# Two reorderings in a transformer block: token sums over other rows, and norms one group of sums later

## The chip, the cores and the metric

The kernel runs on one core of a Trainium2 chip. The metric is the device time of one execution in microseconds, the median of several runs; lower is better. The engines named below are TensorE (PE in the profile; PEld is its weight load), VectorE (DVE), ScalarE (ACT), GpSimd (POOL) and SyncE (SP). The last two, and sometimes ScalarE, also issue transfers between the on-chip memory (SBUF) and DRAM. TensorE writes its results to another on-chip memory, PSUM, from which VectorE or ScalarE takes them.

## The reference

One block of a diffusion transformer, in float32, on `x` of shape (2, 2048, 576) with a condition vector for each of the two sequences. Cut to what matters:

```python
mod = silu(c) @ w_ada + b_ada
sh_msa, sc_msa, g_msa, sh_mlp, sc_mlp, g_mlp = split(mod, 6, axis=1)
xn = ln(x) * (1 + sc_msa) + sh_msa
q, k, v = split_heads(xn @ w_qkv + b_qkv)          # 16 heads of 36
q, k = ln(q), ln(k)
o = softmax(q @ k.T * scale) @ v                   # over all 2048 tokens
x = x + g_msa * (o @ w_proj + b_proj)              # "projection"
xn2 = ln(x) * (1 + sc_mlp) + sh_mlp
h = gelu(xn2 @ w1 + b1)                            # 576 -> 2304
x = x + g_mlp * (h @ w2 + b2)
```

The line marked "projection" and the layer norm of the line after it are what the change concerns.

## The kernel before

The program has two branches; the profiled one is `block_of_small`. It treats the two sequences b = 0 and b = 1 in turn: inputs (norm, q, k, v), attention, projection. Then comes the MLP over all 4096 tokens, in two parts: `w1` with the gelu, whose results go to DRAM, and `w2`. A token tile is 128 rows of 576 numbers; a sequence has 16 tiles. In the MLP a block is 512 tokens. A job makes two slices of 128 hidden features for one block, and does so with seven products of half size in place of eight; there are 8 blocks of 9 jobs.

Instructions of an engine run in the order in which they stand in the program. TensorE's order is the order of the source throughout the branch. VectorE's is the order of the source in the two projections and from the second one to the end; there a list of closures (`between`, `placed`) is the only thing that puts other work into it. ScalarE, GpSimd and SyncE are ordered by a scheduler there. A wait is set for the engine wherever a buffer's last user has to be done, including transfers that still read a buffer which is to be overwritten.

**Projection (`outputs`, L1250 on).** Sixteen tiles in groups of four. For a tile, `whole` (L413) multiplies the attention output by the first 512 rows of `w_proj`, and `halved` (L424) by the last 64. TensorE's order in a group is: `whole` of tiles 0 and 1, `halved` of all four, `whole` of tiles 2 and 3. Each tile takes one of four PSUM buffers, so tile t can start only when tile t-4 has been taken out. For tiles 2 and 3 of a group the first instruction is the `halved` one.

- `evicted` (L1264): VectorE multiplies the PSUM result by the gate into `product`, which frees the PSUM buffer.
- `summed` (L1271): VectorE adds `product` to the residual rows `x1` in SBUF, and GpSimd stores the sum to `x1_dram` (L1272). `residual(t + 6)` loads the rows of a later tile (L1259) into one of nine row buffers.
- In projection 1 (the one of b = 0), the first five tiles are normed at once for the MLP. `rows_measured` takes mean and variance (L272, L274 on VectorE, a square root on ScalarE at L276, a reciprocal on VectorE at L278). `turned` then norms the rows in place (L1280) and transposes them in 32x32 squares (L898), and GpSimd writes the squares to DRAM (L903). L1280 overwrites rows that the store L1272 reads.

In projection 1 the row buffers are parts of `kr` (the name in the profile); in projection 2 they are `x1_rows`, nine tiles x1_0 to x1_8 (the name in the profile is `x`), and tile t lies in buffer t modulo 9.

While projection 1 runs, the weights of the next inputs are loaded by SyncE (L866, L869, L875), and split by VectorE (L407, L408). ScalarE modulates the first two input tiles (L920, L395, L396), with a subtraction on GpSimd (L397).

**Start of the MLP.** The scratch pool with `x1_rows` is closed, and the pool `m1` is opened at the same place in SBUF. It holds the tiles `css` (two of 5120 bytes per partition) and `ss` (three of 2048 bytes). `token_sums` (L1526 to L1529) fills `ss` with sums and differences of token halves, which TensorE takes as moving operands in `whole_part` (L1556). The first job asks first for products that need no sum. `gelu_stored` (L1582 to L1594) puts a job's products together in `css[side]`, applies the gelu and stores the result (L1595). The weights of the second half, `ws`, are loaded by SyncE (L1626), and the gelu results of a block come back through L1637.

Of the kernel before, what the change touches and what calls it, by code (L numbers as in the profile page):

```python
# [8 lines left out]
F32 = mybir.dt.float32  # L9
# [3 lines left out]
ALU = mybir.AluOpType  # L13
# [3 lines left out]
P = 128  # L17
# [14 lines left out]
def dit_block(  # L32
# [25 lines left out]
    nc = tc.nc  # L58
# [27 lines left out]
    def s_tile():  # L86
        return psum["s"].tile([P, 2, 512], F32, tag="s", name="s")
# [8 lines left out]
    def opened(name, bufs=1, side="left"):  # L96

        stack = ExitStack()
        pool = stack.enter_context(tc.tile_pool(name=name, bufs=bufs, side=side, reuse_waits="tile"))
        return pool, stack.close  # L100
# [22 lines left out]
    def halves(ap):  # L123
        return ap.rearrange("p (a f) -> p a f", a=2)
# [144 lines left out]
    def rows_measured(pool, xt):  # L269
        st = pool.tile([P, 2, 6], F32, name="st", bufs=2)  # L270
        for a in range(2):
            nc.vector.bn_stats(st[:, a, :], xt[:, a * HALF : (a + 1) * HALF])  # L272
        mv = pool.tile([P, 2], F32, name="mv", bufs=2)
        nc.vector.bn_aggr(mv, st.rearrange("p a s -> p (a s)"))  # L274
        std = pool.tile([P, 1], F32, name="std", bufs=2)
        nc.scalar.activation(std, mv[:, 1:2], AF.Sqrt, bias=eps6)  # L276
        rstd = pool.tile([P, 1], F32, name="rstd", bufs=2)
        nc.vector.reciprocal(rstd, std)  # L278
        return mv[:, 0:1], rstd
# [8 lines left out]
    with psum_pools(), tc.tile_pool(name="ada", bufs=2) as ada:  # L288
# [19 lines left out]
        turned = s_tile()  # L308
# [101 lines left out]
    def whole(outs, stationary, moving, first):  # L410
        for a in range(2):
            for k in range(FULL):
                nc.tensor.matmul(  # L413
                    outs[a],
                    stationary(k, a),
                    moving(k, a),
                    start=(first and k == 0),
                    stop=(not first and k == FULL - 1),
                )

    def halved(outs, stationary, moving, first):
        for a in range(2):
            r = slice(64 * a, 64 * a + 64)
            nc.tensor.matmul(  # L424
                outs[a], stationary(FULL, a)[r], moving(FULL, a)[r], start=first, stop=not first
            )
# [332 lines left out]
    def block_of_small():  # L759
# [3 lines left out]
        xs = {}  # L763
# [486 lines left out]
        def outputs(b, weights, between, scratch, turned_of=lambda t: None):  # L1250


            wp, wp4, g1, pool = weights
            x1s, to_turn = {}, []

            def residual(t):
                if t < NT:
                    x1s[t] = scratch[t % len(scratch)]
                    nc.gpsimd.dma_start(out=x1s[t], in_=x1_dram[b, t * P : (t + 1) * P, :])  # L1259

            def evicted(ts):
                for t in ts:
                    product = pool.tile([P, C], F32, name="product", bufs=2)
                    nc.vector.tensor_tensor(halves(product), tiles[t % 4][:, :, :HALF], halves(g1), ALU.mult)  # L1264
                    products.append((t, product))

            def summed():
                while products:
                    t, product = products.pop(0)
                    x1 = x1s.pop(t)  # L1270
                    nc.vector.tensor_tensor(x1, x1, product, ALU.add)  # L1271
                    nc.gpsimd.dma_start(out=x1_dram[b, t * P : (t + 1) * P, :], in_=x1)  # L1272
                    residual(t + 6)
                    if turn := turned_of(t):
                        to_turn.append((turn, x1, rows_measured(xs["pool"], x1)))

            def turned():
                while to_turn:
                    turn, x1, scales = to_turn.pop(0)
                    nc.vector.tensor_scalar(x1, x1, *scales, ALU.subtract, ALU.mult)  # L1280
                    turn(x1)

            def placed(t):
                for do in between.get(t, ()):
                    do()

            products = []
            for t in range(6):
                residual(t)
            for t0 in range(0, NT, 4):  # L1290
                tiles, sums = [], []
                for t in range(t0, t0 + 4):
                    if t < t0 + 2:
                        placed(t)
                    ps = s_tile()
                    tiles.append(ps)
                    sums.append((
                        [ps[:, a, :HALF] for a in range(2)],
                        lambda k, a, t=t: qo[:, k, t * P : (t + 1) * P],
                        lambda k, a: wp[:, k, a * HALF : (a + 1) * HALF] if k < FULL else wp4[:, 0, :],  # L1300
                    ))
                    if t < t0 + 2:
                        whole(*sums[-1], True)
                summed()
                for i, sum_ in enumerate(sums):
                    halved(*sum_, i >= 2)
                evicted((t0, t0 + 1))
                turned()
                placed(t0 + 2)
                summed()  # L1310
                whole(*sums[2], False)
                evicted((t0 + 2,))
                turned()
                placed(t0 + 3)
                whole(*sums[3], False)
                evicted((t0 + 3,))
            summed()


# [6 lines left out]
        for b in range(B):  # L1326
# [45 lines left out]
            if b + 1 < B:  # L1372
                begun = [(spare[9 + t], x[b + 1, t * P : (t + 1) * P, :], spare[7 + t]) for t in range(2)]
# [28 lines left out]
            if b + 1 < B:  # L1402
                weights, close_weights = input_weights()
                first_turned, rows = opening["turned"]
                xnt = input_loaded(first_turned, nc.sync)
                first = []

                def turned_of(t):
                    squares = spare[9 + t % 3]
                    return (lambda x1: first.append(squares_turned(x1, nc.gpsimd, squares))) if t <= TPB else None  # L1410

                with tc.manual_schedule(engines={mybir.EngineType.DVE}):
                    outputs(b, wp, {12: [lambda: input_modulated(b + 1, xnt)]}, spare[:9], turned_of)
                close_wp()
# [25 lines left out]
        PAIR = 2 * P  # L1440
# [59 lines left out]
        in_order = tc.manual_schedule(engines={mybir.EngineType.DVE})  # L1500
        in_order.__enter__()
        outputs(B - 1, wp, between, x1_rows)
        close_rows4()
        close_scratch()
# [8 lines left out]
        hidden = [m2.tile([P, NF, PAIR], F32, name="hidden0")]  # L1513
        m1, close_m1 = opened("m1")

        css = [m1.tile([P, 5, PAIR], F32, name=f"cs{i}") for i in range(2)]
        ss = {m: m1.tile([P, 2, PAIR], F32, name=f"s{m}") for m in (1, 2, 4)}
        stack = ExitStack()
        banks = stack.enter_context(tc.tile_pool(name="ps_m", bufs=1, space=PSUM, reuse_waits="tile"))
        ps_m = [banks.tile([P, 3, 512], F32, name=f"m{i}") for i in range(2)]  # L1520
# [245 lines left out]
    with tc.If(is_small > 0) as branch:  # L1766
        with tc.manual_schedule(engines={mybir.EngineType.PE}):
            block_of_small()
# [34 lines left out]
```

## Time and profile before

| what | value |
|---|---|
| median of 3 runs | 3188.86 us (3187.74 to 3190.65) |
| the profiled execution | 3190.46 us |
| its span, first to last instruction | 3188.4 us |
| mean granted TensorE clock | 0.997 |
| `whole` of the two projections, L413 | 512 matmuls, 128.5 us busy, 412 ns each |
| `product`, L1264 | 32, 23.3 us busy, 746 ns each |
| row sums, L1271 | 16 of projection 1: 11.5 us, 744 ns each; 16 of projection 2: 11.5 us, 752 ns each |
| norm in place, L1280 | 5 in projection 1, median 579 ns |
| first token sum, L1526 | 8, 691 ns each |
| row stores, L1272 | 32 of 288 KB |

How to read it: a line of a view names the source line, the engine, the operation, and which tile is made from which (`kr<-kr,product`). "Idle before" is the time for which the engine had nothing running before that instruction, and the name after the arrow is what ended the wait, as far as the semaphores tell. In a timeline the first number is the start in microseconds from the start of the span, the second the duration. `PEclk` is the share of its full clock that TensorE was granted.

### The profile page before, as it was taken

How to read it: one execution, taken by the hardware profiler on the slowest of the kernel's cores; microseconds unless marked ns; L12 is line 12 of the kernel's file. 1: busy time of each engine (PE TensorE's matmuls, PEld its weight loads, DVE VectorE, ACT ScalarE, POOL GpSimd, SP SyncE). 2: the span in 40 equal slices, each digit the busy share in tenths (PEclk: the TensorE clock that was granted, in tenths of full speed). 3: DMA queues.
4: the chain of work that ended last, by engine and by line, in shares of the span. 5: the costliest groups of instructions: out<-in, count | busy, mean ns of one | idle time of the engine just before them, and what ended most of it. 6: DMA issues, size and time to landing. Idle time of an engine off the chain costs nothing. (4 is left out here: it accounts for less than half of the span.)

```text
span 3188.4 us, 47349 instructions
## 1 busy us (share of the span) xinstructions
PE 3157.1 (99%) x17833; PEld 1895.6 (59%) x17833; DVE 1511.4 (47%) x2212; ACT 1514.7 (48%) x2953; POOL 661.8 (21%) x933
## 2 busy tenths in 40 slices
PE   8999999999999999999999999999999999999999
PEld 6884333333333788733333333357888888777777
DVE  5774333333334577633333333345566554455454
ACT  2436666666666034466666666642555642000000
POOL 4551000112110355300001111012333320112111
PEclk9999999999999999999999999999999999999999
DMA  5322212223221633221222223146554433333331
GB/s 151 75 65 69 75 35 69 63 73 83 66 71 43 191 71 71 59 55 43 48 48 65 67 67 75 48 166 185 153 145 131 136 110 143 124 127 112 119 104 38
DMA packets 154537, 290.04 MB, mean 91 GB/s; under 512 B 34419, under 2 KB 86844, under 8 KB 152188
## 3 DMA queue, kind: packets, MB, share of 16 engines
q1 hardware_dynamic: 106212, 170.47, 17.7%
q0 software_dynamic: 44544, 110.85, 13.9%
q10 hardware_dynamic: 3544, 5.60, 0.6%
q8 instruction: 143, 2.34, 0.3%
q14 instruction: 94, 0.77, 0.1%
HBM read 153.95 MB, written 84.63 MB: 75 GB/s over the span
## 5 line engine op out<-in xcount | busy, mean ns | idle before, releaser
L1131 ACT ACTIVATE pt<-b 128x512 f32<-128x512 f32 x2048 | 1057.2, 610 | 486.7 <-PE b L1140 271.1
L1140 PE MATMUL b<-pt,vt 128*64 128x512 f32 x4096 | 935.0, 598 | 0.0
L1140 PEld LDWEIGHTS b<-pt,vt 128*64 128x64 f32 x4096 | 271.8, 136 | 582.0 <-issue 438.8
L1127 PE MATMUL b<-qm,km 32*128 32x512 f32 x4096 | 568.0, 614 | 0.8 <-DVE vt L1044 0.6
L1188 DVE TENSOR_TENSOR ot<-b,ot 128x512 f32<-128x512 f32 x192 | 132.7, 691 | 652.0 <-PE b L1140 651.6
L1127 PE MATMUL b<-qe,ke 16*128 16x512 f32 x2048 | 423.5, 790 | 0.0
L1033 PE MATMUL s<-wq,xnt 128*128 128x288 f32 x1536 | 406.7, 408 | 2.8 <-DMA wq<-in_w_qkv_dram 2.0
L1127 PEld LDWEIGHTS b<-qm,km 32*128 32x128 f32 x4096 | 191.8, 184 | 270.5 <-ACT pt L1131 207.6
L1715 PE MATMUL s<-ws,as 128*128 128x288 f32 x1440 | 351.8, 406 | 0.0
L1033 PEld LDWEIGHTS s<-wq,xnt 128*128 128x128 f32 x1536 | 281.7, 191 | 65.1 <-issue 3.0
L1715 PEld LDWEIGHTS s<-ws,as 128*128 128x128 f32 x1440 | 273.6, 190 | 75.6
L1159 DVE RECIPROCAL den<-den 128x512 f32<-128x512 f32 x64 | 213.5, 3337 | 9.3 <-DMA den<-den_dram 9.3
L1556 PE MATMUL m<-s,wb 128*128 128x256 f32 x864 | 212.4, 382 | 4.3 <-DVE s L1526 4.3
L1556 PE MATMUL m<-xnt,wb 128*128 128x256 f32 x864 | 211.1, 380 | 1.4 <-issue 0.9
L903 POOL DMA_DIRECT2D turned<-squares x220 | 147.6, 677 | 268.8 <-DVE squares L898 245.0
L1186 DVE COPY ot<-b 128x512 f32<-128x512 f32 x64 | 44.3, 692 | 334.0 <-PE b L1140 334.0
L1556 PEld LDWEIGHTS m<-s,wb 128*128 128x128 f32 x864 | 165.7, 192 | 27.6 <-DVE s L1526 4.7
L1127 PEld LDWEIGHTS b<-qe,ke 16*128 16x128 f32 x2048 | 108.3, 184 | 114.4 <-issue 112.9
L1556 PEld LDWEIGHTS m<-xnt,wb 128*128 128x128 f32 x864 | 159.5, 191 | 21.2 <-issue 1.3
L1244 POOL DMA_DIRECT2D kr<-in_x_dram x32 | 17.5, 546 | 727.5 <-DVE met L790 727.5
L1594 ACT ACTIVATE cs<-cs,b_sb 128x512 f32<-128x512 f32 x144 | 98.8, 719 | 118.5 <-DVE cs L1589 98.4
L1715 PE MATMUL s<-ws,hidden 128*128 128x288 f32 x576 | 142.3, 406 | 0.0
(199 smaller groups left out, 3006.0 us busy)
## 6 DMA issues: line engine op xcount, KB each, us to landing
gelu<-cs SPq DMA_DIRECT2D x144, 256.0 KB
hidden<-gelu SPq DMA_DIRECT2D x16, 2304.0 KB
den<-den_dram SPq DMA_DIRECT2D x128, 128.0 KB
turned<-squares POOLq DMA_DIRECT2D x220, 72.0 KB, 2.5
xnt<-turned POOLq DMA_DIRECT2D x56, 256.0 KB, 3.8
x_dram<-kr POOLq DMA_DIRECT2D x48, 288.0 KB, 3.0
qm<-qo SPq DMA_DIRECT2D x192, 64.0 KB
kr<-in_x_dram POOLq DMA_DIRECT2D x34, 288.0 KB, 3.7
```

The source lines that it names most:

```text
L903: queue.dma_start(out=by_square[g], in_=squares[g * SQ : (g + 1) * SQ, :].rearrange("p (k j) -> p k j", j=SQ))
L1033: nc.tensor.matmul(out_a, full[:, k, :], wq[:, k, f], start=k == 0, stop=False)
L1127: nc.tensor.matmul(ps, k[r, keys], q[r, :], start=first, stop=not first)
L1131: nc.scalar.activation(pt[:, h, :], banks[2 * c + h], AF.Exp, scale=SCALE)
L1140: nc.tensor.matmul(acc[64 * h : 64 * h + 64, :], vt[:, v0 : v0 + 64], pt[:, h, :], start=pt is pts[0][0], stop=pt is pts[-1][0],)
L1159: nc.vector.reciprocal(den, den)
L1186: nc.vector.tensor_copy(ot, acc)
L1188: nc.vector.tensor_tensor(ot, acc, ot, ALU.add)
L1244: nc.gpsimd.dma_start(out=spare[t % 2], in_=x[b, t * P : (t + 1) * P, :])
L1556: nc.tensor.matmul(out_m[m], wb[:, slot[m], k, f * P : (f + 1) * P], moving[m](k), start=k == 0 and m in (1, 2, 5, 6), stop=k == 1 and m == 1,
L1594: nc.scalar.activation(part, part, AF.Gelu, bias=b1_sb[:, g : g + 1])
L1715: nc.tensor.matmul(ms[m], stationary[m][:, f, :], ws[m][:, f, :], start=(f == 0), stop=(f == HF - 1))
```

## The change

In `outputs`, the function `turned` goes. What it did (norm in place, transpose, write) is now at the head of `summed`, for the tiles that an earlier `summed` measured. Within one `summed`, all row sums and stores come first and the measurements after them, where before a tile's measurement stood directly after its sum. The two calls of `turned` between the evictions go. In the first pool of the MLP, `ss` is allocated ahead of `css`, so that `ss` lies at the pool's start. What is computed stays the same.

```diff
             def summed():
+                while to_turn:
+                    turn, x1, scales = to_turn.pop(0)
+                    nc.vector.tensor_scalar(x1, x1, *scales, ALU.subtract, ALU.mult)
+                    turn(x1)
+                begun = []
                 while products:
                     t, product = products.pop(0)
                     x1 = x1s.pop(t)
...
                     nc.gpsimd.dma_start(out=x1_dram[b, t * P : (t + 1) * P, :], in_=x1)
                     residual(t + 6)
                     if turn := turned_of(t):
-                        to_turn.append((turn, x1, rows_measured(xs["pool"], x1)))
-
-            def turned():
-                while to_turn:
-                    turn, x1, scales = to_turn.pop(0)
-                    nc.vector.tensor_scalar(x1, x1, *scales, ALU.subtract, ALU.mult)
-                    turn(x1)
+                        begun.append((turn, x1))
+                for turn, x1 in begun:
+                    to_turn.append((turn, x1, rows_measured(xs["pool"], x1)))
...
                 evicted((t0, t0 + 1))
-                turned()
                 placed(t0 + 2)
                 summed()
                 whole(*sums[2], False)
                 evicted((t0 + 2,))
-                turned()
                 placed(t0 + 3)
...
+        ss = {m: m1.tile([P, 2, PAIR], F32, name=f"s{m}") for m in (1, 2, 4)}
         css = [m1.tile([P, 5, PAIR], F32, name=f"cs{i}") for i in range(2)]
-        ss = {m: m1.tile([P, 2, PAIR], F32, name=f"s{m}") for m in (1, 2, 4)}
```

## The prediction

> **What bounds the kernel now.** I read the page first (busy time), then TensorE's waits over the span, then the timeline around the two waits that the diff can touch, and last the granted clock in short windows there.
>
> ```profile
> span 3188.4 us, 47349 instructions
> PE 3157.1 (99%) x17833; PEld 1895.6 (59%) x17833; DVE 1511.4 (47%) x2212; ACT 1514.7 (48%) x2953; POOL 661.8 (21%) x933
> ```
>
> TensorE is busy all the time, VectorE half of it. So only what makes TensorE stand still, or run slowly, can be won. Its waits (us in total, times, longest):
>
> ```profile
> PE s L310 <- DVE x_first L283: 8.4, 1, 8.4
> PE m L1556 <- DVE s L1526: 4.3, 1, 4.3
> PE s L424 <- DVE product L1264: 2.7, 1, 2.7
> ```
>
> The first is in the setup, which the diff leaves alone. The second and third are its two places. Place 1, projection 1 of the first sequence (start, duration, instruction, idle before):
>
> ```profile
> 1067.27 0.58 DVE L1280 TENSOR_SCALAR kr<-kr,mv,rstd 128x576 f32<-128x576 f32 x1 [3.73 <-DMA x_dram<-kr]
> ...
> 1069.29 0.64 DVE L1280 TENSOR_SCALAR kr<-kr,mv,rstd 128x576 f32<-128x576 f32 x1 [0.62 <-DMA x_dram<-kr]
> ...
> 1074.95 1.73 PE L424 MATMUL s<-wp,qo 64*128 64x288 f32 x12
> ...
> 1077.29 0.58 DVE L1280 TENSOR_SCALAR kr<-kr,mv,rstd 128x576 f32<-128x576 f32 x1 [2.90 <-DMA x_dram<-kr]
> 1077.90 0.78 DVE L898 STREAM_TRANSPOSE kr<-kr 128x576 f32<-128x576 f32 x1
> 1078.61 0.72 DVE L1264 TENSOR_TENSOR product<-s,gate 128x576 f32<-128x576 f32 x1
> ...
> 1079.38 0.76 PE L424 MATMUL s<-wp,qo 64*128 64x288 f32 x4 [2.71 <-DVE product L1264]
> 1080.07 17.48 PE L413 MATMUL s<-wp,qo 128*128 128x288 f32 x64
> ```
>
> L1280 norms tile 4's rows in place, so it waits until their store (issued at 1074.29) has read them; the product of tile 7 is behind it, TensorE needs tile 7's bank for tile 11, and stands. Place 2, the start of the MLP:
>
> ```profile
> 2181.08 1.21 POOL L1272 DMA_DIRECT2D x_dram<-x  x2 [7.51 <-DVE x L1271]
> ...
> 2182.02 1.03 PE L1556 MATMUL one<-xnt,wb 128*128 128x256 f32 x4
> ...
> 2186.57 0.69 DVE L1526 TENSOR_TENSOR s<-xnt 128x512 f32<-128x512 f32 x1 [5.12 <-DMA x_dram<-x]
> 2187.31 3.06 PEld L1556 LDWEIGHTS m<-s,wb 128*128 128x128 f32 x8 [4.67 <-DVE s L1526]
> ```
>
> The first token sum waits for the stores of tiles 14 and 15, whose rows lay where `ss` lies now. The wait costs more than itself, as the clock shows (PE, PEld, DVE, ACT, POOL busy, then granted clock):
>
> ```profile
> 1081.00:1082.00 1.00, 1.00 (x4) 0.71 (x3) 1.00 (x3) 0.00 (x0) 1.00 (x3) 0.50 0.75 172
> ...
> 2188.00:2189.00 1.00, 1.00 (x4) 0.82 (x3) 1.00 (x3) 0.00 (x0) 0.00 (x0) 0.50 1.09 379
> ```
>
> [...] 0.50 from about 1081 to 1084 and from 2187 to 2193. [...] what stands behind L1280 waits with it, as L1264 did at 1078.61. [...] the store issued at 1062.00, beside the weight loads, landed 7.26 us later (L1280 starts on it at 1069.29); one issued at 1074.29, without them, took 2.9.
>
> **Place 2, the swap of `ss` and `css`.** The tiles lie over `x1_rows`, nine rows of 2304 bytes. Before, css takes bytes 0 to 10240 and ss 10240 to 16384, over rows 4 to 7, which held tiles 13, 14 and 15 last. After, ss takes 0 to 6144, over rows 0 to 2, tiles 9 to 11 last. Their stores were issued at 2168.53 at the latest, and by the trace's landing records were in by 2174.7. So L1526 can follow the last row sum on VectorE, at about 2181.5, and its result is there at 2182.2; TensorE asks for it after the four `one` matmuls, at 2182.9. L1527 to L1529 follow at 0.6 to 0.7 us each, the last result at 2184.2, asked for at 2185.5. No wait is left. css is now over tiles 11 to 15: ScalarE writes the first half at 2183, after the landing of tile 13 at 2176.2; the second is written by job 1, near 2194, and tile 15 landed at 2187.7. Cost nothing.
> A job of the MLP takes 7.00 us (from 2201.88 to 2208.88, the timeline's first L1556 groups). The first one starts at 2180.22 and the second at 2194.88: 14.66. Saving 14.66 - 7.00 = 7.66: 4.3 of waiting, the rest half clock. After that the MLP is TensorE's alone: its largest wait there is 0.5 us, near 2279, behind gelu stores and a 2.3 MB load which start when job 8 has stored, so they move along. What begins 7.7 us nearer to the third `ws` load (2181.48 to about 2190) is the first transposed rows, L903; their rows land 3.5 us before ScalarE takes them (L913 2205.0, L395 2208.5), of which I expect to lose 2.
>
> **Place 1, the order in `summed`.** Nothing is added: five L1280, L898 and five measurements as before. Moved: the norms of a pair stand after the products of the next two tiles, directly ahead of the next two row sums; a pair's two sums come before its measurements. On the other queues: the stores of tiles 0 and 1 become neighbours on GpSimd, and L397 for both input tiles stands before the eight L903 issues, not after them; ScalarE's square roots and L920 change places; SP's order is the same.
> I walk VectorE with the row durations and the old DMA delays.
> - Up to 1050: both sums by 1045.4, both measurements by 1049.0, products 2 and 3 by 1050.5 (3 was at 1052.92). L1280 for tiles 0 and 1 then waits a little for stores that went out at 1044.9 and 1045.5. Sums 2 and 3 end at 1054.6.
> - L407 waits for the bias load as before, to 1057.80; only the idle before it grows, from 0.67 to about 2.5. The casts end at 1062.06, then the measurement of tile 3 (1.6) and products 4 and 5, to 1065.1. TensorE wants bank 4 at 1067.1: 2 us spare.
> - GpSimd: L397 twice needs ScalarE's L396 twice. The rows land at about 1050.7 (L911 goes out 0.57 later than 1045.45), and L920, L395, L396 and L397 take some 3.8, so the L903 issues start at 1054.5 to 1055, not 1053.59. The stores of tiles 2 and 3 wait behind them (at 1061.43 for the landings of the first two L903; the VectorE instruction named there had nothing to do with their rows). So store 3 goes out up to 1.4 later; but the bulk load ends by 1070 whatever the order. Its landing, 1069.26 before, I bound by 1069.3 and 1070.7, and take 1070.0.
> - From L1280 of tile 3 to the end of product 7 are now L1280 and L898 (1.38), two sums (1.45), a measurement (1.56) and two products (1.39), from start to start in the old timeline: 5.8 together. So product 7 is ready at 1075.1 to 1076.5. TensorE wants it at 1076.55, twelve L424 after 1074.95. The wait is nothing, at the worst a few tenths.
> - L1280 of tile 4 waits for its store to about 1078, with sums 6, 7 and products 8, 9 behind it, done at 1082.5; TensorE wants bank 8 at 1085.1. That cover is 2.6 us; were it gone, each us costs one.
> From one first L424 to the next is 17.86 undisturbed (1057.09 to 1074.95) and 22.52 here (1074.95 to 1097.47): saving 4.66. From 1107 to the MLP TensorE has no wait over 1.4 us and the weights landed by 1070, so it carries through.
> **Sum:** 4.66 + 7.66 = 12.3, bounds 10 (place 1 keeps a wait of up to 1.7 us, place 2 loses 0.6) and 12.4. The profiled execution took 3190.46 (span 3188.4, 2.1 around it): 3178.1. The median of the three runs is 1.6 lower: 3176.6.
>
> **Rivals.**
> - The wait of place 1 only changes place: store 3 lands later than 1070.7 and L1280 holds products 6 and 7 as long as before. For: two more instructions' worth of work stands between them now, and stores beside loads took 7 us. Against: the slack above. Place 2 alone: 3188.9 - 7.7 = 3181.2.
> - Place 2 brings nothing: another landing ends L1526's wait, or the stores and loads near 2276 end at a fixed time and TensorE waits 8 us there instead of 0.5. For: the chain of waits runs through them for 13 us. Against: they are issued by the MLP's own jobs. Place 1 alone: 3184.2.
> - Neither moves the end: 3188.9.
> - Slower: the norm of tile 3 heads VectorE's queue, ahead of two sums, a measurement and both products. Each us that store 3 lands after 1070.8 is a us of TensorE, plus 1.7 at half clock. It must land 10.6 late, at 1081.4, to eat 12.3; at 1088.5 the time is 3196. Against: no row store of that stretch took over 7.3 us.
>
> **How the numbers follow.** Both places 0.78; place 2 alone 0.08; place 1 alone 0.06; neither 0.04; slower 0.04. A measurement tells 0.2% (6.4 us) from no change; 3182.5 is the limit. Faster: 0.78 + 0.08 = 0.86; same: 0.06 + 0.04 = 0.10; slower 0.04. The likeliest case's own bounds, 10 and 12.4, with 1.5 us of spread between runs either way, give 3175 to 3180.5; the range goes to 3182 to take in place 2 alone, and to 3174 below.
>
> **What would show it.** L424 after `product` gone from TensorE's waits, and 17.9 us between those groups; no granted 0.50 at 1081; L1526 at 2181.5 without idle; first MLP job 7.0 us. Wrong would be: L1280 of tile 3 starting after 1070.8, a new TensorE wait on `product`, or a longer wait on `cs` in the MLP's second ten jobs.

## The result, and the profile after

| | before | after |
|---|---|---|
| median | 3190.65 us (9 runs, 3187.74 to 3195.2) | 3179.67 us (9 runs, 3177.61 to 3185.67) |
| ratio | | 0.997, 95% interval 0.9959 to 0.998 |
| the profiled execution, its span | 3190.46, 3188.4 us | 3178.22, 3176.4 us |
| place 1: from one first L424 to the next | 22.52 us | 17.96 us |
| place 2: first job of the MLP | 14.66 us | 7.08 us |

In the changed kernel's profile L1280 is L1270, the row sum L1271 is L1276, its store L1272 is L1277, and what stands below is one line lower (L1556 is L1555). From its page, the span, and busy time by engine:

```profile
span 3176.4 us, 47350 instructions
...
PE 3152.3 (99%) x17833; PEld 1892.8 (60%) x17833; DVE 1511.0 (48%) x2212; ACT 1515.4 (48%) x2953; POOL 670.3 (21%) x933
```

Each engine has as many instructions as before. TensorE's 4.8 us less of busy time (3157.1 before) fits the matmuls that no longer run at half clock: before had 10.2 us of it at the two places, and half of that, 5.1 us, is time lost. TensorE's waits after (total, times, longest):

```profile
PE s L310 <- DVE x_first L283: 8.2, 1, 8.2
PE s L1033 <- DMA wq<-in_w_qkv_dram: 2.8, 1, 2.8
PE b L993 <- ACT pt L1131: 1.4, 1, 1.4
PE m L1555 <- issue: 0.9, 1, 0.9
```

Both waits that the prediction named, L424 for `product` and the s matmuls for L1526, are gone from the list. Place 1 after, from the timeline (start, duration, instruction, idle before):

```profile
1058.74 5.58 POOL L903 DMA_DIRECT2D turned<-kr  x8 [2.90 <-DVE wq L407]
...
1065.34 0.59 POOL L1277 DMA_DIRECT2D x_dram<-kr  x1 [1.03 <-DVE product L1264]
1066.25 0.55 POOL L1277 DMA_DIRECT2D x_dram<-kr  x1 [0.32 <-issue]
...
1070.43 0.58 DVE L1270 TENSOR_SCALAR kr<-kr,mv,rstd 128x576 f32<-128x576 f32 x1 [5.24 <-DMA x_dram<-kr]
...
1071.74 0.54 DVE L1270 TENSOR_SCALAR kr<-kr,mv,rstd 128x576 f32<-128x576 f32 x1
...
1073.02 1.38 DVE L1276 TENSOR_TENSOR kr<-kr,product 128x576 f32<-128x576 f32 x2
...
1075.78 2.32 PE L424 MATMUL s<-wp,qo 64*128 64x288 f32 x16
...
1075.88 1.40 DVE L1264 TENSOR_TENSOR product<-s,gate 128x576 f32<-128x576 f32 x2
1077.34 0.30 PEld L424 LDWEIGHTS s<-wp,qo 64*128 64x128 f32 x4 [0.29 <-DVE product L1264]
```

Two products now run one directly after the other, and the sixteen L424 take 2.32 us in one piece. But look at the last line: the weight load still waited 0.29 us for the product. The norm of tile 2 started late, when its store had landed, and everything behind it on VectorE came just in time. The margin is used up. Place 2 after:

```profile
2176.34 1.42 DVE L1276 TENSOR_TENSOR x<-x,product 128x576 f32<-128x576 f32 x2
...
2176.53 1.97 PE L1555 MATMUL m<-xnt,wb 128*128 128x256 f32 x8 [0.90 <-issue]
...
2177.68 0.69 DVE L1525 TENSOR_TENSOR s<-xnt 128x512 f32<-128x512 f32 x1
...
2179.20 1.89 PE L1555 MATMUL m<-s,wb 128*128 128x256 f32 x8
```

The token sum follows the last row sum without idle, 0.8 us ahead of the matmul that takes it.

### The profile page after: what moved, and what is told of

The parts are those of the page before. It is cut to its first block, busy times and chain, and to the rows that moved or that the text cites. A ratio compares the mean times of both kernels' runs of the same rounds, so it can differ in the third digit from the quotient of the medians.

```text
span 3176.4 us, 47350 instructions
## 1 busy us (share of the span) xinstructions
PE 3152.3 (99%) x17833; PEld 1892.8 (60%) x17833; DVE 1511.0 (48%) x2212; ACT 1515.4 (48%) x2953; POOL 670.3 (21%) x933
## 4 chain that ended last, share of the span: by engine, by line
PE 98%; DVE 1%; DMA 1%; SPq 0%; ACT 0%; issue 0%; ACTq 0%; DVEq 0%
PE b L1140 29%; PE b L1127 19%; PE s L1714 15%; PE m L1555 12%; PE s L1033 11%; PE s L413 4%; PE m L1569 2%; PE one L1555 2%; PE s L1035 1%; PE s L993 1%; PE s L424 1%; DMA bq<-in_w_qkv_dram 0%; DMA wq<-in_w_qkv_dram 0%; PE b L192 0%; DVE var L973 0%; DMA km<-qo 0%
## 5 line engine op out<-in xcount | busy, mean ns | idle before, releaser
L1127 PE MATMUL b<-qm,km 32*128 32x512 f32 x4096 | 568.1, 614 | 0.9 <-DVE vt L1044 0.6
L1127 PE MATMUL b<-qe,ke 16*128 16x512 f32 x2048 | 423.7, 790 | 0.0
L1127 PEld LDWEIGHTS b<-qm,km 32*128 32x128 f32 x4096 | 192.3, 184 | 270.5 <-ACT pt L1131 208.4
L1555 PE MATMUL m<-xnt,wb 128*128 128x256 f32 x864 | 210.2, 379 | 0.9 <-issue 0.9
L1555 PE MATMUL m<-s,wb 128*128 128x256 f32 x864 | 210.0, 379 | 0.0
L903 POOL DMA_DIRECT2D turned<-squares x220 | 148.3, 680 | 258.7 <-DVE squares L898 235.3
L1555 PEld LDWEIGHTS m<-s,wb 128*128 128x128 f32 x864 | 164.2, 190 | 22.3
L1127 PEld LDWEIGHTS b<-qe,ke 16*128 16x128 f32 x2048 | 108.3, 184 | 114.4 <-issue 113.1
L1555 PEld LDWEIGHTS m<-xnt,wb 128*128 128x128 f32 x864 | 158.9, 190 | 20.3 <-issue 1.3
```

The source lines that it names most:

```text
L903: queue.dma_start(out=by_square[g], in_=squares[g * SQ : (g + 1) * SQ, :].rearrange("p (k j) -> p k j", j=SQ))
L1127: nc.tensor.matmul(ps, k[r, keys], q[r, :], start=first, stop=not first)
L1555: nc.tensor.matmul(out_m[m], wb[:, slot[m], k, f * P : (f + 1) * P], moving[m](k), start=k == 0 and m in (1, 2, 5, 6), stop=k == 1 and m == 1,
```

## The experiments

The measure is the stage, not only the total: the totals of one kernel spread over some 4 to 12 us, and most of the differences asked about are smaller. The timelines give, for each profile: the start of the L424 group before place 1 (what came before the change's first place), the interval at place 1, the time from its end to the MLP's first matmul, and the first MLP job. The windows of 1 us give how long the clock was 0.50 in each. The three d_ runs are single executions.

| kernel | start | place 1 | to the MLP | first job | half clock: place 1, second attention, place 2 | median us (runs) |
|---|---|---|---|---|---|---|
| before | 1057.09 | 22.52 | 1082.75 | 14.66 | 3.41, 0, 6.82 | 3190.65 (9) |
| after | 1057.92 | 17.96 | 1082.79 | 7.08 | 0, 0, 0 | 3179.67 (9) |
| e_order | 1059.22 | 18.65 | 1086.53 | 13.06 | 0, 10.24, 3.41 | 3186.48 (13) |
| e_swap | 1057.28 | 22.61 | 1084.27 | 7.08 | 3.41, 3.41, 0 | 3182.64 (21) |
| e_apart | 1055.35 | 17.86 | 1086.48 | 7.07 | 0, 10.24, 0 | 3179.14 (5) |
| e_sync | 1054.88 | 17.86 | 1087.12 | 7.07 | 0, 10.24, 0 | 3183.23 (13) |
| d_low | 1058.56 | 19.91 | 1084.25 | 9.30 | 0, 3.41, 0 | 3185.15 (1) |
| d_mid | 1058.15 | 22.90 | 1084.18 | 12.44 | 3.41, 3.41, 3.41 | 3191.13 (1) |
| d_high | 1055.58 | 24.80 | 1084.09 | 13.77 | 6.82, 3.41, 3.41 | 3191.18 (1) |
| e_rows | 1055.65 | 18.10 | 1080.98 | 7.07 | 0, 0, 0 | 3175.52 (5) |
| e_rows_apart | 1058.90 | 17.86 | 1080.93 | 7.08 | 0, 0, 0 | 3176.11 (5) |
| e_rows_sync | 1056.29 | 18.41 | 1080.92 | 7.07 | 0, 0, 0 | 3175.42 (5) |
| b_rows | 1056.84 | 19.82 | 1081.15 | 13.10 | 0, 0, 3.41 | 3186.51 (21) |
| again | 1058.77 | 19.06 | 1086.07 | 7.08 | 0, 6.82, 0 | 3183.09 (6) |

The kernel before, run beside them, had medians of 3189.84 (41 runs), 3191.29 (9) and 3190.26 (26). The stage that the table leaves out, from the second MLP job to the end, takes 1010.4 to 1011.9 us in all fourteen profiles. But the start, ahead of the change's first place, already differs by 4.3 us.

**e_order: place 1 alone.** The order in `summed` is the changed one, the allocation the old one.

```diff
-        ss = {m: m1.tile([P, 2, PAIR], F32, name=f"s{m}") for m in (1, 2, 4)}
         css = [m1.tile([P, 5, PAIR], F32, name=f"cs{i}") for i in range(2)]
+        ss = {m: m1.tile([P, 2, PAIR], F32, name=f"s{m}") for m in (1, 2, 4)}
```

> Only place 1 is changed (the order in `summed`); ss and css are allocated as before. My theory, two independent waits each with its own half clock: 4.6 us less than the kernel before, ratio 0.9986 (0.9980 to 0.9992); TensorE's wait L424 <- product is gone or under 0.7 us, the interval between the two L424 groups is 17.9 to 18.6, and the wait of the MLP's first s matmul stays at 4.3 us with the clock at 0.50 after it. Rival, the whole gain is place 2's: ratio 1.000. Rival, the gains are not additive (the MLP waits for something that ends at a fixed time): ratio near 0.997, or near 1.000.

Ratio 0.9991, interval 0.9983 to 0.9999: a gain, smaller than the 4.6 us expected, which lies inside the interval. From the timeline of e_order:

```profile
1077.87 1.40 DVE L1264 TENSOR_TENSOR product<-s,gate 128x576 f32<-128x576 f32 x2
1078.66 0.30 PEld L424 LDWEIGHTS s<-wp,qo 64*128 64x128 f32 x4 [0.80 <-DVE product L1264]
1078.66 1.42 PE L424 MATMUL s<-wp,qo 64*128 64x288 f32 x8 [0.34 <-DVE product L1264]
...
2189.34 3.48 PE L1555 MATMUL m<-s,wb 128*128 128x256 f32 x8 [4.25 <-DVE s L1525]
```

A small wait of 0.34 us is left at place 1. Place 2 has its wait of 4.25 us, as before; yet its first job takes 13.06 us, not 14.66. For the same wait the half clock lasted 3.41 us here and 6.82 there.

**e_swap: place 2 alone.** The kernel before, with `ss` ahead of `css`.

> Only place 2 is changed (ss before css); `summed` is as before. My theory: 7.6 us less than the kernel before, ratio 0.9976 (0.9968 to 0.9984); the wait on s is gone, the first MLP job takes 7.0 to 7.2 us, and TensorE still stands 2.7 us for the product in projection 1 with the clock at 0.50 after it. Rival, the gain is lost near the gelu stores of job 9: ratio 1.000.

Ratio 0.9979, interval 0.9972 to 0.9986; both stages as expected (22.61 and 7.08). So place 2 does not need place 1, nor place 1 place 2 (e_order), and nothing near the gelu stores takes the gain back.

**e_apart: no norm waits for a store.** What spread the changed kernel's runs over 8 us? My first theory was the thin margin.

```diff
-                    nc.vector.tensor_scalar(x1, x1, *scales, ALU.subtract, ALU.mult)
-                    turn(x1)
+                    nc.vector.tensor_scalar(spare[8], x1, *scales, ALU.subtract, ALU.mult)
+                    turn(spare[8])
...
-                    outputs(b, wp, {12: [lambda: input_modulated(b + 1, xnt)]}, spare[:9], turned_of)
+                    outputs(b, wp, {12: [lambda: input_modulated(b + 1, xnt)]}, spare[:8], turned_of)
```

> The changed kernel, with the norm of a residual row written to a ninth row (eight rows in turn hold the residuals), so that no norm waits for the landing of its row's store. Theory: the changed kernel's place 1 has no slack left (product 7 was ready just when TensorE asked), so its slower executions (3183 to 3186 us, granted clock 0.996 to 0.997) are those in which store 3 lands late and TensorE stands; here they go: all executions within 3177 to 3180, clock 0.999, median 3178, ratio to before 0.9963. VectorE has no idle before L1270, and product 7 is ready 4 us or more before TensorE asks. Rival, the slower executions have another cause (elsewhere on the core): they stay, with the same spread, and the median is that of the changed kernel, 3179.7.

Place 1 is undisturbed: both products end at 1070.28, ahead of the L424 group itself at 1073.21. The theory fell all the same: runs from 3175.77 to 3180.49, and the profiled one has a mean clock of 0.997. In this profile the time went in the stage between, where the second attention starts (middle figure of the half clock column). In the total the median, 3179.14, is not to be told from the changed kernel's.

**e_sync: the stores out of the queue behind the transposed rows.**

```diff
-                    return (lambda x1: first.append(squares_turned(x1, nc.gpsimd, squares))) if t <= TPB else None
+                    return (lambda x1: first.append(squares_turned(x1, nc.sync, squares))) if t <= TPB else None
```

> The changed kernel, with the transposed rows of projection 1 written out from SyncE's queue instead of GpSimd's, so that the stores of tiles 2 and 3 no longer stand behind them. Theory: the stores of tiles 2 and 3 are issued at 1054 to 1056 instead of 1065.3 and 1066.3, land by 1066 although the weights are still loading, and VectorE does not wait for them; product 7 is ready 3 us or more early; times as in the kernel with the norm apart, 3177 to 3180. Rival, it is the weight loads and not the queue that delay the landing: they land at 1069 to 1071 as before, and the time and its spread are the changed kernel's.

A miss in the time: 3183.23, slower than the changed kernel's first median. From VectorE's timeline in e_sync:

```profile
1064.22 0.58 DVE L1270 TENSOR_SCALAR kr<-kr,mv,rstd 128x576 f32<-128x576 f32 x1 [3.09 <-DMA x_dram<-kr]
...
1066.02 0.58 DVE L1270 TENSOR_SCALAR kr<-kr,mv,rstd 128x576 f32<-128x576 f32 x1 [0.40 <-DMA x_dram<-kr]
1069.18 0.78 DVE L898 STREAM_TRANSPOSE kr<-kr 128x576 f32<-128x576 f32 x1 [2.58 <-DMA turned<-kr]
...
1072.74 1.40 DVE L1264 TENSOR_TENSOR product<-s,gate 128x576 f32<-128x576 f32 x2
```

The stores do go out earlier (1057.13 and 1057.67) and land by 1064.2 and 1066.0; with this profile's start 3.04 us ahead of after's, that is 3.2 and 2.1 us earlier. But now a transpose waits 2.58 us for the transposed rows on SyncE's queue, and the products are ready no earlier against the L424 group than in after. The interval is the undisturbed 17.86, so in this profile the loss lies elsewhere: 4.3 us between place 1 and the MLP. Whether the kernel is slower at all is open, for the changed kernel's own second median is 3183.09 (next).

**again: the changed kernel once more.**

> The changed kernel once more, beside the others on one chip. Median 3179.7, executions in two heaps, near 3178 and near 3183, according to whether the wait at the second attention (1.36 us in each) is followed by half clock. If its profile is of the slower kind, the clock is 0.50 at 1331 to 1345 and the two stages of the change stand at 17.9 to 18.7 and 7.1.

The two heaps came, two runs near 3177.8 and four from 3182.5 to 3184.4, but the median of 3179.7 did not: it was 3183.09, ratio 0.9973, interval 0.9961 to 0.9985. Its profile is of the longer kind. The start of the second attention in it:

```profile
1332.78 0.53 ACTq L1467 DMA_DIRECT2D last_rows<-in_w_dram  x1
1333.50 1.28 ACT L1131 ACT_TABLE_LOAD   x1 [1.81 <-DMA qm<-qo]
1334.79 4.03 ACT L1131 ACTIVATE pt<-b 128x512 f32<-128x512 f32 x8
...
1335.53 0.74 PE L993 MATMUL b<-ident,both 128*128 128x128 f32 x5 [1.36 <-ACT pt L1131]
```

ScalarE issues a transfer, `last_rows`, ahead of the first exponentials; they come late, and TensorE stands 1.36 us. That wait is 1.35 to 1.37 us in every profile without the edit below, those of before and after too. What follows it differs. The windows of again (length, busy PE, PEld, DVE, ACT, POOL, granted clock, DMA share, GB/s):

```profile
1337.00:1338.00 1.00, 1.00 (x10) 0.60 (x9) 0.99 (x4) 1.00 (x3) 0.05 (x1) 1.00 0.97 208
1338.00:1339.00 1.00, 1.00 (x12) 0.80 (x11) 0.84 (x2) 0.82 (x2) 0.00 (x0) 0.59 1.04 183
1339.00:1340.00 1.00, 1.00 (x13) 0.92 (x7) 0.00 (x0) 0.25 (x1) 0.00 (x0) 0.50 1.05 193
```

Here 6.82 us at half clock follow; in the profiles of before and after none; in three others 10.24. The stage to the MLP takes 1082.8 us with none, 1084.2 with 3.41, 1086.1 with 6.82 and 1086.5 to 1087.1 with 10.24. The expectation allowed up to 18.7 for place 1; it was 19.06, with 0.75 us of waiting for `product`, the longest interval of this order without a dose.

**e_rows: that transfer from another queue.** `last_rows` is read first at 2139, some 800 us later.

```diff
-        nc.scalar.dma_start(out=last_rows, in_=w1[512:576, :].rearrange("p (a f) -> p a f", a=2))
+        nc.sync.dma_start(out=last_rows, in_=w1[512:576, :].rearrange("p (a f) -> p a f", a=2))
```

> The changed kernel, with one transfer issued from SyncE's queue instead of ScalarE's: last_rows (L1467), which in the trace stands on ScalarE just ahead of the second attention's first exponentials and waits there; TensorE's 1.36 us wait L993 <- pt follows from it. Theory: this wait is the source of most of the spread between runs (four of six profiles have 3.4 to 10 us at half clock after it, the other two none, for the same 1.36 us): the wait shrinks below 0.5 us, the half clock at 1331 to 1345 is gone in all executions, all within 3175 to 3179.5, median 3176.8, ratio to before 0.9957. Rival, the spread comes from the setup, where TensorE waits 1.6 to 5 us for the weights of the first sequence: spread as in the changed kernel, median 1.4 less (3178.3).

In e_rows the same stretch reads:

```profile
1327.61 1.28 ACT L1131 ACT_TABLE_LOAD   x1
...
1328.90 4.03 ACT L1131 ACTIVATE pt<-b 128x512 f32<-128x512 f32 x8
1329.62 0.52 SPq L1467 DMA_DIRECT2D last_rows<-in_w_dram  x1
...
1330.01 0.77 PE L993 MATMUL b<-ident,both 128*128 128x128 f32 x5
```

The wait for `pt` is gone, the stage takes 1.8 us less, and no half clock is left in it. Ratio to before 0.9955, interval 0.9941 to 0.9968; runs from 3174.53 to 3178.11. The interval overlaps that of the changed kernel (0.9959 to 0.998); the runs taken together, below, tell the two apart.

**e_rows_apart, e_rows_sync, b_rows: the same edit on other kernels** (with e_apart's edit, with e_sync's, and on the kernel before).

> The norm apart in a ninth row and last_rows from SyncE's queue, together. Theory: no thin margin at place 1, no wait at the second attention: median as with last_rows alone, 3176 to 3177.5, spread not over 4 us; never a half clock after 1060. Rival, the thin margin at place 1 costs nothing in most executions: no difference from last_rows alone beyond 0.5 us.

> last_rows and the transposed rows of projection 1 both from SyncE's queue. With the transposed rows alone on it the median was 3183.2, against 3179.7 of the changed kernel, though its interval between the L424 groups was the undisturbed 17.86; its profile lost 4.3 us between the first L424 groups and the MLP, all after the 1.36 us wait of the second attention. Theory: that wait and its half clock are the whole difference, so with last_rows moved the median is 3175.5 to 3177, as with last_rows alone. Rival: the transposed rows on SyncE's queue delay something else: 3178.5 or more.

> The kernel before, with last_rows issued from SyncE's queue and nothing else. Theory: the wait at the second attention is independent of the change: 1.8 us less in every execution and 2 to 4 more in those that had the half clock; median 3186.5 (3185.5 to 3188), ratio 0.9988; both waits of the change's places stand as before. Rival: [...] what is won at 1331 is lost at 2187: ratio 0.9995 or more.

e_rows_apart: 3176.11, ratio 0.9951 (0.9937 to 0.9964), not to be told from e_rows; its runs spread over 5 us, one more than expected. What spread is left fits the rival named for e_rows, the setup: the profile of e_rows_apart took 2.57 us more than that of e_rows and reached the start 3.25 us later. TensorE's wait for the first weights differs by about as much (e_rows, then e_rows_apart):

```profile
PE s L1033 <- DMA wq<-in_w_qkv_dram: 1.7, 1, 1.7
PE s L1033 <- DMA wq<-in_w_qkv_dram: 4.2, 2, 3.7
```

No run changed the setup, so this is not shown by experiment.

e_rows_sync: 3175.42, ratio 0.9957 (0.9943 to 0.997), four of five runs within 0.6 us, one at 3180.45, for which there is no profile. So the transposed rows on SyncE's queue cost nothing that shows once the second attention's wait is gone.

b_rows: 3186.51, ratio 0.999 (0.9983 to 0.9997), as expected: this edit gains on the old kernel about as much as place 1 does (e_order, 0.9991). The three variants with the new order have 15 runs with a median of 3175.4; the changed kernel, with those of again, 15 with 3180.6. Both waits of the change's places were expected to stand as before; place 1 came out milder:

```profile
1074.70 1.73 PE L424 MATMUL s<-wp,qo 64*128 64x288 f32 x12
1078.11 0.76 PE L424 MATMUL s<-wp,qo 64*128 64x288 f32 x4 [1.69 <-DVE product L1264]
1094.52 2.21 PE L424 MATMUL s<-wp,qo 64*128 64x288 f32 x16
```

The wait is 1.69 us, not 2.71, no half clock follows, and the interval is 19.82.

**d_low, d_mid, d_high: waits by hand.** What does a wait cost beyond itself? The changed kernel, with VectorE made late at both places. What is computed stays the same; the low dose is shown, the others have 3 and 6, and 5 and 8 repeats more than the changed kernel.

```diff
-                    nc.vector.tensor_tensor(halves(product), tiles[t % 4][:, :, :HALF], halves(g1), ALU.mult)
+                    for _ in range(3 if b == 0 and t == 6 else 1):
+                        nc.vector.tensor_tensor(halves(product), tiles[t % 4][:, :, :HALF], halves(g1), ALU.mult)
...
-            nc.vector.tensor_tensor(ss[1], a10, a11, ALU.add)
+            for _ in range(5 if n == 0 else 1):
+                nc.vector.tensor_tensor(ss[1], a10, a11, ALU.add)
```

> The changed kernel with VectorE made late by hand at both places: the product of tile 6 in projection 1 of the first sequence is computed three times instead of once (2 x 0.67 = 1.3 us), the first token sum of the MLP's first block five times instead of once (4 x 0.61 = 2.4 us). Place 1 has no slack in the changed kernel: TensorE should stand 1.1 to 1.6 us for the product; place 2 has 0.7 us of it: TensorE should stand 1.6 to 2.0 us for s. Theory, [...] each place loses its idle alone (interval between the L424 groups 19.3, first MLP job 8.9) or its idle and 1.7 to 5 us more. Rival, an idle below 2.7 us never halves the clock: 19.3 and 8.9 exactly, granted clock 1.00 at both. Rival, the price is always 1 us and 1.7 more per us: 21 and 12.

> Doses between the low and the high: three repeats of the product, six of the token sum. Idles of 2.3 to 2.7 us at place 1 and 3.1 to 3.5 at place 2. The doses so far: 1.70 and 1.96 of idle cost themselves alone, 2.71 cost 3.4 us at half clock besides, 4.3 to 4.9 between 3.4 and 6.8. Theory, half clock comes in pieces of about 3.4 us [...]: each place loses its idle, or its idle and about 1.7 us; nothing between. Rival, the price grows evenly with the idle: place 1 0.5 to 1.0 us over its idle, place 2 1.0 to 1.5.

> As the low dose, with five repeats more of the product (3.3 us) and eight more of the token sum (4.9 us). TensorE should stand 3.0 to 3.6 us for the product and 4.0 to 4.4 us for s, both longer than the 2.7 that cost 3.4 us at half clock in the kernel before. Theory: clock 0.50 at both; interval between the L424 groups 17.9 + 3.3 + 1.7 to 3.5 = 22.9 to 24.7; first MLP job 7.1 + 4.2 + 1.7 to 3.5 = 13 to 14.8. Rival, the half clock of the kernel before came from what stood beside the waits and not from the idle: 21.2 and 11.3 at a clock of 1.00.

The waits were 1.70, 3.04 and 4.32 us at place 1, and 1.96, 3.42 and 4.87 at place 2. From d_low's timeline (the added lines move L1264 to L1265 and L1555 to L1557):

```profile
1079.36 1.33 PE L424 MATMUL s<-wp,qo 64*128 64x288 f32 x8 [1.70 <-DVE product L1265]
...
2185.37 1.99 PE L1557 MATMUL m<-s,wb 128*128 128x256 f32 x8 [1.96 <-DVE s L1527]
```

Both cost little more than themselves: 19.91 is 2.05 over the undisturbed 17.86, and 9.30 is 2.22 over 7.08, with the clock at 1.00 throughout. In d_mid both cost 3.41 us at half clock besides (22.90 and 12.44). In d_high the wait of 4.32 brought 6.82 and the longer one, 4.87, only 3.41. The price does not grow evenly with the wait. It comes in pieces, as d_mid's windows show:

```profile
1081.00:1082.00 1.00, 1.00 (x7) 0.51 (x6) 0.49 (x1) 0.00 (x0) 0.00 (x0) 0.69 0.99 235
1082.00:1083.00 1.00, 1.00 (x3) 0.71 (x3) 0.97 (x3) 0.00 (x0) 0.00 (x0) 0.50 1.01 383
...
1084.00:1085.00 1.00, 1.00 (x4) 0.65 (x4) 1.00 (x3) 0.00 (x0) 1.00 (x2) 0.60 0.67 143
1340.00:1341.00 1.00, 1.00 (x5) 0.66 (x4) 1.00 (x4) 1.00 (x4) 0.28 (x1) 0.90 0.86 180
1344.00:1345.00 1.00, 1.00 (x9) 0.20 (x3) 0.00 (x0) 0.30 (x1) 0.00 (x0) 0.90 0.15 51
2190.00:2191.00 1.00, 1.00 (x6) 0.88 (x5) 1.00 (x3) 0.00 (x0) 0.00 (x0) 0.85 1.07 386
2194.00:2195.00 1.00, 1.00 (x7) 0.87 (x7) 0.14 (x1) 0.00 (x0) 0.56 (x1) 0.94 1.09 362
```

A mean clock of 0.69 in a window of 1 us is 0.62 us at half clock, so the first piece began at 1081.38; in the same way it ended at 1084.80, and the others run from 1340.80 to 1344.20 and from 2190.70 to 2194.12. Each lasts 3.40 to 3.42 us. Their starts lie 259.42 and 849.90 us apart, which is 76.0 and 249.0 times 3.4133. That length is an estimate, fitted to the starts in the traces. In each of the five profiles with more than one such stretch from place 1 on (before, e_order, e_swap, d_mid, d_high) the starts lie whole multiples of it apart, within 0.02 us. So do those in the setup of before: at 19.24 and 32.90, they are 311.0 and 307.0 such lengths ahead of the one at 1080.80. Why the pieces lie so, no run tells.

## Why the prediction was right, and where not

**Place 2, right.** L1525 started without idle and the first job took 7.08 us against 7.0. No landing took the wait's place, and `css` over the later rows cost TensorE nothing. The transposed rows of the MLP's start came late, as expected (L920, at 2197.59, waited 1.78 us for them), also without cost to TensorE. The predicted 7.66 was the profile's gain, and 7.58 came; but 7.66 held one draw of the half clock. Where it lasted one piece and not two (e_order, b_rows) the first job took 13.06 and 13.10, and the gain is 6.0. The half clock is not a fixed 1.7 us (half of one piece of 3.41), as the rival for slower had it. Beyond the wait itself a place lost 0.3 us where the clock held (d_low), 1.9 to 2.0 with one piece of half clock (d_mid), and 3.3 with two (before, place 2).

**Place 1, right in kind, thin in margin.** The predicted saving was 4.66, and 4.56 came. Behind it the walk was off at two steps, and by luck it cost almost nothing. First, GpSimd's writes L903 were put at 1054.5 to 1055; they came at 1058.74, on a timeline 0.83 us later, so about 3 us late. GpSimd idled 2.90 us ahead of them, and the stores of tiles 2 and 3 went out at 1065.34 and 1066.25, by the old timeline 3.1 and 3.4 us later than before, where "up to 1.4" was predicted. But the landing of store 3 moved far less than its issue: it came at 1071.10, which is 1070.27 on the old timeline, 1.0 later than before and inside the 1069.3 to 1070.7 given. This is what the prediction argued from the weight loads; that it is the loads which set it is not shown, since no run took them away. Second, the walk left out store 2. Its landing moved from 1067.27 (where L1280 starts on it) to 1070.43 (L1270) and started the chain; store 3 landed while tile 2 was still being normed and transposed. So the norm of tile 3 started at 1071.74, on the old timeline 1070.91: just past the 1070.8 that the prediction had named as a sign of being wrong. From there to the end of product 7 the prediction had 5.8 us; it was 5.54, and this gave back enough for product 7 to be ready when TensorE asked. In the six profiles with this order and no dose, other than those with the norm apart, the interval is 17.96, 18.65, 17.86, 18.10, 18.41 and 19.06. In three profiles of the old order it is 22.52, 22.61 and 19.82. The bound of "a wait of up to 1.7 us" was needed.

**The term that was off: from the profiled execution to the median.** The sum was made on one profile, 3178.1, and the profile of after took 3178.22. Part of that agreement is luck too: the two places gave 12.1 us, the start was 0.8 later, and the rest of the MLP, from its second job on, 0.7 shorter. Then 1.6 was taken off because the median of three runs lay so much below the profile; 41 runs of the kernel before later had a median of 3189.84, only 0.6 below it. And both profiles were draws without half clock at the second attention; all eight others that keep `last_rows` on ScalarE's queue had it, at 1.4 to 4.3 us each. By the medians the gain is 11.0 us (3190.65 less 3179.67), where 12.3 was predicted. In again it was 7.2 us (3190.26 less 3183.09), and that median lies outside the predicted 3174 to 3182. So the two places gave what was forecast, stage by stage; that the first median fell well inside the range was in part a lucky draw, of a spread that the prediction had put at 1.5 us either way.

**The rivals.** The wait of place 1 changing place is excluded as a whole by the intervals of the new order and of the old, just given; e_order's 0.9991, with an interval that ends at 0.9999, agrees but would not carry it alone. In part it is what the thin margin shows. That place 2 brings nothing is excluded by e_swap; the wait near 2279 on which that rival rested was 0 to 1.14 us in every profile. That neither moves the end is excluded by the result, 0.997 with an interval below 1. For the slower case the norm of tile 3 did stand at the head of VectorE's queue; its landing, 1070.27 against the 1081.4 that would have eaten the gain, was 11 us short of deciding anything.

**Open.** Why GpSimd idles 2.5 to 2.9 us ahead of its first transfer in that stretch, for which the trace shows no cause: it names VectorE's cast L407 in after and e_sync, whose result those transfers don't use, and nothing in e_apart. It stood before L903 in after and e_apart, and before a residual load in e_sync, each time beside the weight loads. For most of it, in after and e_apart, VectorE was idle too. No run took the loads away.

## What to carry to other kernels

When a buffer is reused, put the part that is written first over the rows whose transfers were issued first; here such a swap of two allocations gave 7.6 us of the first job without an instruction less. When an in-place operation waits for a store, the operation in another buffer (e_apart) takes the landing out of the account, where a later place in the queue only moves the margin; here the stage was then undisturbed (17.86 us), though the total did not show it. And when runs of one kernel differ by a fixed few microseconds, compare profiles stage by stage: the largest cause here was one transfer at the head of ScalarE's queue, whose data was wanted 800 us later.

## What the hardware showed

The half clock came in pieces of 3.41 us, up to three in a row (10.24). TensorE's waits for `product` at place 1 and for the token sum at place 2, by the half clock that came with each:

| half clock, us | place 1, wait in us | place 2, wait in us |
|---|---|---|
| 0 | 0.34 (e_order), 0.75 (again), 1.69 (b_rows), 1.70 (d_low) | 1.96 (d_low) |
| 3.41 | 2.71 (before), 2.79 (e_swap), 3.04 (d_mid) | 3.42 (d_mid), 4.25 (e_order), 4.34 (b_rows), 4.87 (d_high) |
| 6.82 | 4.32 (d_high) | 4.27 (before) |

No run has a wait between 1.96 and 2.71 there. How many pieces come cannot be told from the length of a wait: two came with 4.27, one with 4.87. What sets their number was not shown.

At the second attention the length of the wait does not tell even whether a piece follows: the same 1.35 to 1.37 us was followed by none to three. The windows of after, again and e_apart there, each about one piece long (length, busy PE and so on as above):

```profile
1330.99:1334.40 3.41, 1.99 (x16) 0.94 (x15) 0.03 (x1) 2.83 (x5) 3.41 (x5) 1.00 0.87 242
1334.77:1338.18 3.41, 2.50 (x15) 1.73 (x16) 1.84 (x6) 3.40 (x9) 2.28 (x5) 1.00 0.91 217
1334.15:1337.57 3.42, 3.42 (x21) 2.30 (x13) 0.65 (x2) 1.13 (x3) 0.00 (x0) 0.50 0.66 131
```

In after, 1.42 us of waiting in 3.41 us brought no half clock. In again the half clock began at 1338.18, at the end of 3.41 us with 0.91 of waiting. In e_apart it went on from 1337.57 to 1340.98, though TensorE was never idle in the 3.42 us before, where place 1 of the kernel before had the full clock back after one piece. What stands there are matmuls of 32 and 16 rows (L1127, 614 and 790 ns each in before); whether those rows are the reason no run tells.
